# A selective-scan kernel: B products of four states at once in four row groups, and all decays in SBUF

## The chip, the cores and the metric

The kernel runs on one core of one Trainium2 chip. The metric is device time in microseconds, the median of three runs. A profiled execution is a further run with the hardware profiler on; its time and its trace are used for the parts.

## What is computed

Two layers over an image tensor of 16 x 64 x 64 x 128, in float32. Layer 0 is a two-dimensional LSTM, with a group norm ahead and a residual. Layer 1, where the change is, is a bidirectional Mamba block with the same dress. It flattens each image to 4096 tokens and runs this, once forward and once on the reversed tokens:

```python
dt, Bm, Cm = jnp.split(dbl, [DT_RANK, DT_RANK + D_STATE], axis=-1)
dt = jax.nn.softplus(dt @ dt_w.T + dt_b)
dA = jnp.exp(dt[..., None] * A)
dBx = dt[..., None] * Bm[:, :, None, :] * xc[..., None]
def step(h, inp):
    dA_t, dBx_t, C_t = inp
    h = dA_t * h + dBx_t
    return h, jnp.einsum('bds,bs->bd', h, C_t)
...
y = (ys + xc * D) * jax.nn.silu(z)
return y @ out_w.T
```

There are 256 inner channels (two halves `h` of 128 partitions) and 16 states. For each channel and state the recurrence over the tokens needs a decay `dA`, a driving term `dBx` (the "B product"), and afterwards a product with C, summed over the states.

## The kernel before

Layer 0 walks the anti-diagonals of the images. Its cell (lines 833 to 865) multiplies gates and states on VectorE, and one of these products on GpSimd (L859), with both operands in SBUF; L841, L860 and L862 are such VectorE products.

Layer 1 works in passes of T = 512 tokens: 8 chunks per direction, 16 passes per image, 256 in all. A pass holds channels in partitions and tokens in columns. ScalarE makes a decay for every state and half (`decay`, L1217: exp of dt times a per-partition scale). VectorE runs the recurrence of one state and half as one scan over 512 columns (`scan`, L1277), 32 scans per pass. A scan has two tensor operands, the decay and the driving term, and starts from `carry`, which small transfers fill (`keep`, `keep_group`).

The states are treated in two ways.

- X states (0 to 7): GpSimd multiplies dt times x (`dtx`) by rows of B spread over the partitions, for two states at a time, into an SBUF tile `group` of four states (`drive`, L1225). The decay goes to a PSUM bank `da`. The scan overwrites its part of `group`. PE turns the finished group (`turned`, L1307), ScalarE copies it out to `ht` (L1315), and PE weighs it with C (`weigh`, L1323, four column groups).
- R states (8 to 15): PE makes the driving term as a product of the turned `dtx` (`dtxt`) and a matrix `d` with rows of B on its diagonals (`drive_rows`, L1257), for two states at once, in two row groups of 64 tokens, into a PSUM tile `pair` of two banks (named `hps` in the trace). The decay goes to SBUF (`das`). The scan writes to SBUF (`hst`). GpSimd multiplies it by rows of C (`out_of`, L1300), and PE sums it (`sums`).

A pass so has 17 GpSimd products: 8 drives, 8 outs and `dtx` (`times`, L1191), each of 1024 columns.

PSUM has eight banks: four in a common store, of which at most two hold decays and two anything else (`LIMIT`), two for `pair`, which the dt projection uses as well, and two for the sum `py`. SP issues the transfers: spread rows of B and C, the matrices `d` and `k`, the scatters that fill them in DRAM, and the carries.

The order of the instructions on every engine is written out at build time. `order_of_issue` lists the operations of all passes with their dependencies and buffers, and `simulate` issues them in a model of the five queues with the durations of `COST`, the ready operation with the lowest due time (`URGENCY` plus 16 per pass) first. Scans keep the order of the string `ORDER`: a digit stands for one X state, a letter for a pair of R states. Each engine then runs its list in order; tile semaphores guard the buffers, whose numbers stand in `RINGS`.

Of the kernel before, what the change touches and what calls it, by code (L numbers as in the profile page):

```python
# [8 lines left out]
F32 = mybir.dt.float32  # L9
# [5 lines left out]
P = 128  # L15
# [21 lines left out]
GX = 4  # L37
TB = P // GX
NX = 8
NG, NR = NX // GX, (NS - NX) // 2  # L40
WD = T + P
ORDER = ("00a00b11c11d22e22f33g33h", "00a00b11c11d22e22f33g33h")


def units_of(order):

    count = {}
    for x in order:
# [3 lines left out]
        else:  # L52
# [4 lines left out]
    "bank": 4, "pair": 1, "py": 1, "das": 3, "dg": 3, "group": 3, "cd": 2, "ht": 6, "hst": 3, "hc": 4,  # L57
    "br": 3, "cr": 2, "xc": 2, "dt": 2, "dtx": 2, "dtxt": 2, "dbl": 2, "z": 1, "y": 1,
# [4 lines left out]
    "conv": 0.865, "gate": 0.87, "silu": 0.62, "softplus": 0.65, "gate_take": 0.6, "dtproj": 1.07,  # L63
    "xproj": 1.0, "xproj_take": 0.4, "times": 2.34,
    "turn": 0.47, "turn_take": 0.47, "decay": 0.62, "drive": 2.34, "drive_rows": 1.08,
    "scan": 1.18, "keep": 0.6, "keep_group": 0.6, "out": 2.34, "sums": 0.88, "skip": 0.44,
    "turned": 0.44, "turned_take": 0.47, "weigh": 1.08,
    "again": 0.88, "finish": 1.0, "finish_last": 1.2, "back": 0.47, "back_take": 0.47,
    "project": 0.95, "store_take": 0.6, "residual": 0.6, "read_load": 0.6, "read_turn": 0.47,
    "read_take": 0.5, "read_stats": 0.62, "normal": 3.0, "normalise": 0.75, "spread": 0.6, "rows": 1.2,  # L70
# [4 lines left out]
LIMIT = {"misc": 2, "bank": 2}  # L75
AHEAD = 3
ROW = 0.9
# [4 lines left out]
        {(0, 0): -5.27, (0, 1): -61.96, (0, 2): -1.51, (0, 3): -31.9, (1, 0): -36.36, (1, 1): -34.22, (1,  # L82
         2): -4.82, (1, 3): -3.48},
        {(0, 0): -13, (0, 1): -15.31, (0, 2): -17.47, (0, 3): -12.25, (1, 0): -17.78, (1, 1): -17.99, (1,
         2): -18.46, (1, 3): -13.31},
    ),
    "xproj": (
        {(): 55.58},
        {(): 50.35},
    ),  # L90
    "xproj_take": (
        {(): -34.19},
        {(): -67.81},
    ),
    "rows": (
        {(): 14.85},
        {(): 29.35},
    ),
    "dtproj": (
        {(): 21.81},  # L100
        {(): 49.19},
    ),
    "times": (
        {(): -216.85},
        {(): -50.5},
    ),
    "turn": (
        {(0,): -139.83, (1,): -112.3},
        {(0,): 38.45, (1,): 39.27},
    ),  # L110
    "turn_take": (
        {(0,): -82.61, (1,): -85.08},
        {(0,): -121.61, (1,): -124.32},
    ),
    "skip": (
        {(0,): -30.72, (1,): -29.27, (2,): -28.89, (3,): -30.37},
        {(0,): -31.71, (1,): -38.35, (2,): -27.4, (3,): -32.33},
    ),
    "spread": (
        {("b", 0): 48.76, ("d", 0): -27.02, ("c", 0): -72.82, ("b", 1): -39.91, ("k", 0): 25.29, ("d",  # L120
         1): -25.84, ("c", 1): 91.24, ("b", 2): 203.69, ("d", 2): 42.8, ("c", 2): -76.57, ("b", 3): 83.9,
         ("k", 1): -178.37, ("d", 3): 47.98, ("c", 3): -120.82},
        {("b", 0): -102.07, ("d", 0): 101.39, ("c", 0): -127.37, ("b", 1): 201.12, ("k", 0): -7.75, ("d",
         1): -16.19, ("c", 1): 237.63, ("b", 2): 27.93, ("d", 2): 187.94, ("c", 2): 178.25, ("b", 3):
         59.58, ("k", 1): 33.49, ("d", 3): -19.86, ("c", 3): 49.53},
    ),
    "drive": (
        {(0, 0): -37.87, (1, 0): -232.55, (0, 1): 70.61, (1, 1): 81.52, (2, 0): 92.85, (3, 0): -81.77,
         (2, 1): 90.65, (3, 1): -60.19},
        {(0, 0): 71.45, (1, 0): 100.65, (0, 1): 69.84, (1, 1): 238.34, (2, 0): -85.16, (3, 0): 16.29, (2,  # L130
         1): 152.24, (3, 1): 151.41},
    ),
    "decay": (
        {(0, 0): -100.09, (1, 0): -113.38, (8, 0): -17.88, (9, 0): -17.98, (2, 0): 115.94, (3, 0):
         -173.37, (8, 1): 117.83, (9, 1): 117.76, (0, 1): 117.57, (1, 1): -199.13, (10, 0): -76.99, (11,
         0): -4.35, (2, 1): -207.87, (3, 1): -174.5, (10, 1): -57.93, (11, 1): 144.9, (4, 0): -62.8, (5,
         0): 9.44, (12, 0): -249.7, (13, 0): -4.82, (6, 0): -90.12, (7, 0): -89, (12, 1): 112.66, (13,
         1): -89.33, (4, 1): -92.07, (5, 1): -92.07, (14, 0): -87.45, (15, 0): -79.99, (6, 1): -83.78,
         (7, 1): -65.02, (14, 1): -92.12, (15, 1): -92.18},
        {(0, 0): -107.74, (1, 0): 78.08, (8, 0): 64.21, (9, 0): 60.4, (2, 0): 66.94, (3, 0): -168.8, (8,  # L140
         1): -38.24, (9, 1): 83.45, (0, 1): -165.22, (1, 1): -93.49, (10, 0): -104.1, (11, 0): 17.18, (2,
         1): 7.23, (3, 1): -108.8, (10, 1): 238.21, (11, 1): -142.57, (4, 0): 16.12, (5, 0): 79.59, (12,
         0): 187.77, (13, 0): -57.05, (6, 0): 11.51, (7, 0): -45.79, (12, 1): 48.63, (13, 1): 3.55, (4,
         1): 76.92, (5, 1): 79.55, (14, 0): 84.29, (15, 0): -45.77, (6, 1): 8.28, (7, 1): 1.52, (14, 1):
         78.29, (15, 1): 80.29},
    ),
    "scan": (
        {(0, 0): -191.9, (1, 0): -180.93, (8, 0): 59.29, (9, 0): 58.95, (2, 0): 47.07, (3, 0): 1.2, (8,
         1): 43.31, (9, 1): 42.72, (0, 1): 139.84, (1, 1): 85.46, (10, 0): 88.15, (11, 0): -220.11, (2,
         1): 67.38, (3, 1): 69.08, (10, 1): 3.2, (11, 1): -48.38, (4, 0): -148.38, (5, 0): -142.6, (12,  # L150
         0): -158.76, (13, 0): -146.42, (6, 0): -147.36, (7, 0): -134.74, (12, 1): -175.53, (13, 1):
         71.17, (4, 1): 33.69, (5, 1): 137.17, (14, 0): 92.55, (15, 0): 96.04, (6, 1): 94.32, (7, 1):
         102.78, (14, 1): 86.19, (15, 1): 71.66},
        {(0, 0): -48.3, (1, 0): -50.57, (8, 0): -47.99, (9, 0): -52.26, (2, 0): -45.52, (3, 0): -48.53,
         (8, 1): -128.37, (9, 1): -157.26, (0, 1): -63.33, (1, 1): -80.02, (10, 0): -74.43, (11, 0):
         -109.52, (2, 1): -66.59, (3, 1): -80.53, (10, 1): 9.22, (11, 1): -125.5, (4, 0): -93.94, (5, 0):
         3.58, (12, 0): 2.78, (13, 0): -27.3, (6, 0): 34.58, (7, 0): 18.59, (12, 1): 6.11, (13, 1):
         12.29, (4, 1): 11.19, (5, 1): 13.36, (14, 0): 20.12, (15, 0): 47.53, (6, 1): 63.73, (7, 1):
         24.81, (14, 1): -31.39, (15, 1): -31.89},
    ),  # L160
    "scatter": (
        {("d", 0): -127.75, ("k", 0): -48.3, ("d", 1): 125.59, ("d", 2): 30.9, ("k", 1): -11.07, ("d",
         3): 59.14},
        {("d", 0): -28.6, ("k", 0): -67.41, ("d", 1): -108.16, ("d", 2): -133.73, ("k", 1): -94.37, ("d",
         3): -129.9},
    ),
    "drive_rows": (
        {(0, 0): 26.17, (0, 1): -3.25, (1, 0): -50.93, (1, 1): -31.58, (2, 0): -0.9, (2, 1): 17.32, (3,
         0): 80.19, (3, 1): -2.75},
        {(0, 0): 33.35, (0, 1): 87.4, (1, 0): -31.34, (1, 1): 14.65, (2, 0): 33.69, (2, 1): 74.37, (3,  # L170
         0): 149.93, (3, 1): -83.5},
    ),
    "keep": (
        {(0, 0): -27.42, (0, 1): -63.13, (1, 0): -50.2, (1, 1): 26.86, (2, 0): 11.68, (2, 1): 92.99, (3,
         0): -130.98, (3, 1): -233.75},
        {(0, 0): -235.44, (0, 1): 51.58, (1, 0): 122.52, (1, 1): 76.67, (2, 0): 102.66, (2, 1): -10.28,
         (3, 0): 48.92, (3, 1): -97.12},
    ),
    "out_of": (
        {(0, 0): 59.79, (0, 1): 61.42, (1, 0): -184.01, (1, 1): -237.54, (2, 0): -19.88, (2, 1): -39.04,  # L180
         (3, 0): 15.92, (3, 1): -83.32},
        {(0, 0): 46.75, (0, 1): 3.87, (1, 0): 82.21, (1, 1): 206.76, (2, 0): 148, (2, 1): -37.11, (3, 0):
         94.4, (3, 1): 76.66},
    ),
    "sums": (
        {(0, 0): 41.95, (0, 1): 68.64, (1, 0): 88.31, (1, 1): 50.57, (2, 0): 73.72, (2, 1): 76.8, (3, 0):
         -112.6, (3, 1): 161.24},
        {(0, 0): 22.75, (0, 1): 60.23, (1, 0): 33.88, (1, 1): 40.44, (2, 0): 217.19, (2, 1): 108.14, (3,
         0): 79.41, (3, 1): 83.91},
    ),  # L190
    "keep_group": (
        {(0, 0): -57.74, (0, 1): 14.03, (1, 0): 44.89, (1, 1): 61.89},
        {(0, 0): -23.9, (0, 1): -25.46, (1, 0): -99.2, (1, 1): -131.55},
    ),
    "turned": (
        {(0, 0, 0): 7.49, (0, 0, 1): -48.32, (0, 0, 2): -49.41, (0, 0, 3): 27.18, (0, 1, 0): 30.12, (0,
         1, 1): 23.21, (0, 1, 2): 38.21, (0, 1, 3): 37.84, (1, 0, 0): 60.1, (1, 0, 1): 19.71, (1, 0, 2):
         91.82, (1, 0, 3): -28.89, (1, 1, 0): 50.64, (1, 1, 1): 50.33, (1, 1, 2): 64.2, (1, 1, 3): 154.68},
# [16 lines left out]
        {(0, 0): 103.15, (0, 1): 79.93, (1, 0): 103.9, (1, 1): 79.84},  # L215
    ),
    "finish": (
        {(): -99.64},
        {(): -37.02},
    ),  # L220
    "spill": (
# [1250 lines left out]
```

## Time and profile before

| what | before |
|---|---|
| median of three runs | 14339.09 us (14334.58 to 14341.66) |
| profiled execution, its own time | 14002.73 us |
| its span | 14000.9 us |
| PE busy | 13085.1 us, 93% |
| VectorE (DVE) busy | 11100.8 us, 79% |
| ScalarE (ACT) busy | 10791.8 us, 77% |
| GpSimd (POOL) busy | 10438.0 us, 75% |
| mean granted PE clock | 0.973 |
| moved by DMA | 1936.5 MB, mean 138 GB/s |

Busy times are of one execution and overlap. Layer 0 fills roughly the first 1500 us, where GpSimd has little to do; after that the pattern of a pass repeats, and a stretch of it shows how near each engine is to the period. In a group's row stand the line, engine and operation, output and inputs with their tiles, the count, busy time and mean duration, and after the second bar the idle time of the engine just before such instructions, with what ended it. In the timeline a row has start, duration, engine, line and operation; "x2" means two merged instructions. PE's LDWEIGHTS and MATMUL are recorded separately, and a float32 product leaves two matmul records. Matmuls overlap, so the cost of one is its group's busy time by its count, not its mean duration.

### The profile page before, as it was taken

What the parts mean: (1) busy time and instruction counts of PE and PEld (TensorE: products, weight loads), DVE (VectorE), ACT (ScalarE), POOL (GpSimd) and SP (SyncE); (2) the same over time, 40 slices, a digit from 0 to 9 for tenths busy, and PEclk for the clock granted to TensorE, in tenths of its full rate; (3) what the DMA queues carried; (4) which work ended last, traced back from release to release, by engine and by line L of the source; (5) the groups of instructions that cost most, each with busy time, mean ns of one, the idle gap of its engine ahead of it and who ended that gap; (6) DMA issues with size and microseconds to landing.
All of it is one profiled execution on the core that took longest, in us unless ns stands there. A gap on an engine that the chain in (4) does not pass through costs nothing. (4 is left out here: it accounts for less than half of the span.)

```text
span 14000.9 us, 315690 instructions
## 1 busy us (share of the span) xinstructions
PE 13085.1 (93%) x124724; PEld 10060.3 (72%) x124724; DVE 11100.8 (79%) x11281; ACT 10791.8 (77%) x17599; POOL 10438.0 (75%) x4612
## 2 busy tenths in 40 slices
PE   8999899898999999998989999998989999998989
PEld 7666667676767777676767777776767677776767
DVE  6776678787887878787878888787878888787878
ACT  3444678788888878787888888788888888787877
POOL 0111488788878888887878888888878888888888
PEclk9999899999999999999999999999999999999999
DMA  4221356565555556565655555565655556565655
GB/s 144 56 57 51 84 144 156 137 152 141 152 146 147 149 144 152 137 156 141 152 142 150 149 146 147 143 158 141 151 144 153 144 149 146 143 156 142 152 141 140
DMA packets 3787992, 1936.50 MB, mean 138 GB/s; under 512 B 2938624, under 2 KB 3284240, under 8 KB 3786512
## 3 DMA queue, kind: packets, MB, share of 16 engines
q1 hardware_dynamic: 3708560, 1881.06, 53.2%
q10 hardware_dynamic: 77952, 35.24, 1.1%
q8 instruction: 986, 16.15, 0.5%
q14 instruction: 494, 4.05, 0.1%
HBM read 1754.87 MB, written 164.89 MB: 137 GB/s over the span
## 5 line engine op out<-in xcount | busy, mean ns | idle before, releaser
L1300 POOL TENSOR_TENSOR hc<-hst,cr 128x1024 f32<-128x1024 f32 x2048 | 4872.9, 2384 | 1497.8 <-DMA cr<-rows 1017.3
L1277 DVE TENSOR_TENSOR_SCAN hst<-das,carry,hps 128x512 f32<-128x512 f32 x3584 | 4376.8, 1262 | 1308.0 <-PE hps L1257 837.8
L1225 POOL TENSOR_TENSOR group<-dtx,br 128x1024 f32<-128x1024 f32 x2048 | 4898.5, 2406 | 403.3 <-DMA br<-rows 251.2
L1277 DVE TENSOR_TENSOR_SCAN group<-da,carry,group 128x512 f32<-128x512 f32 x3584 | 4393.1, 1263 | 463.9 <-ACT da L1217 324.2
L1217 ACT ACTIVATE das<-dt,A_log_sb 128x512 f32<-128x512 f32 x4096 | 2852.3, 724 | 744.5 <-DVE hst L1277 720.8
L1315 ACT COPY ht<-ptg 128x512 f32<-128x512 f32 x4096 | 2263.4, 588 | 890.9 <-PE ptg L1307 868.4
L1217 ACT ACTIVATE da<-dt,A_log_sb 128x512 f32<-128x512 f32 x4096 | 2766.5, 688 | 72.7 <-DVE group L1277 66.5
L1335 PE MATMUL py<-ident,hc 128*128 128x128 f32 x16384 | 2162.0, 281 | 495.7 <-POOL hc L1300 495.1
L1307 PE MATMUL ptg<-ident,group 128*128 128x128 f32 x16384 | 2415.1, 283 | 178.8 <-ACT ht L1315 153.6
L1257 PEld LDWEIGHTS hps<-d,dtxt 64*128 64x128 f32 x32768 | 2050.7, 192 | 636.6 <-issue 486.6
L1257 PE MATMUL hps<-d,dtxt 64*128 64x128 f32 x32768 | 2448.2, 290 | 21.8 <-ACT dt L1182 12.1
L1335 PEld LDWEIGHTS py<-ident,hc 128*128 128x128 f32 x16384 | 1869.3, 144 | 808.3 <-POOL hc L1300 532.5
L1307 PEld LDWEIGHTS ptg<-ident,group 128*128 128x128 f32 x16384 | 1820.5, 143 | 584.4 <-ACT ht L1315 252.5
L1093 PE MATMUL pp<-xT,wk 128*128 128x512 f32 x4096 | 1930.1, 609 | 0.5 <-DVE xl L880 0.5
L1093 PEld LDWEIGHTS pp<-xT,wk 128*128 128x128 f32 x4096 | 733.8, 192 | 735.1 <-issue 688.9
L859 POOL TENSOR_TENSOR a_f<-a_f,c 128x288 f32<-128x288 f32 (+40 forms) x254 | 212.7, 837 | 1331.0 <-ACT a_f L851 1265.9
L1323 PE MATMUL py<-ht,k 128*32 128x128 f32 x32768 | 1114.5, 277 | 0.3 <-ACT ht L1315 0.3
L1323 PEld LDWEIGHTS py<-ht,k 128*32 128x32 f32 x32768 | 837.4, 110 | 197.5 <-issue 177.4
L1191 POOL TENSOR_TENSOR dtx<-dt,xc 128x1024 f32<-128x1024 f32 x256 | 604.1, 2360 | 318.8 <-ACT dt L1182 291.0
L1277 DVE TENSOR_TENSOR_SCAN hst<-das,hps 128x512 f32<-128x512 f32 x512 | 595.4, 1201 | 237.0 <-PE hps L1257 201.2
L1217 ACT ACT_TABLE_LOAD x527 | 676.1, 1283 | 10.2 <-DVE hst L1277 0.4
L1277 DVE TENSOR_TENSOR_SCAN group<-da,group 128x512 f32<-128x512 f32 x512 | 596.0, 1202 | 68.9 <-ACT da L1217 63.7
(110 smaller groups left out, 11834.4 us busy)
## 6 DMA issues: line engine op xcount, KB each, us to landing
cr<-rows SPq DMA_DIRECT2D x1024, 512.0 KB
br<-rows SPq DMA_DIRECT2D x1024, 512.0 KB
d<-d SPq DMA_DIRECT2D x1024, 320.0 KB
k<-k SPq DMA_DIRECT2D x512, 256.0 KB
yf<-yo SPq DMA_DIRECT2D x128, 512.0 KB
yl<-yf SPq DMA_DIRECT2D x128, 512.0 KB
xs<-in_x_dram SPq DMA_DIRECT2D x64, 512.0 KB
d<-rows SPq DMA_DIRECT2D x2048, 2.0 KB
```

Source lines behind the costliest of these rows:

```text
L859: nc.gpsimd.tensor_mul(f0, f0, cp[:, up, :])
L1093: nc.tensor.matmul(self.ps["conv", h], lhsT=wk[:, k, h * P : (h + 1) * P], rhs=xT[self.b % 2][:, t0 : t0 + T], start=(k == 0), stop=(k == ...
L1191: nc.gpsimd.tensor_mul(self.dtx, self.dt, self.xc)
L1217: nc.scalar.activation(t, self.dt[:, h, :], AF.Exp, scale=amat[:, h, s : s + 1])
L1225: nc.gpsimd.tensor_mul(both[:, m : m + 2, :], bc(self.dtx[:, h, :], 1, 2), self.brow[q])
L1257: nc.tensor.matmul(half[:, j, :, :], lhsT=self.dtxt[rows, j, h * P : (h + 1) * P], rhs=dg[rows, j + r, :, :], start=True, stop=True, skip_ ...
L1277: nc.vector.tensor_tensor_scan(t[:, self.rev], self.da.pop((s, h))[:, self.rev], dbx[:, self.rev], 0.0 if self.first else carry[:, self.d, ...
L1300: nc.gpsimd.tensor_mul(self.hc[g, h], self.hst[g, h], self.crow[g])
L1307: nc.tensor.transpose(pt[:, k, :], self.group[g, h][:, t0 : t0 + TB, :].rearrange("p t s -> p (t s)"), ident,)
L1315: nc.scalar.copy(t, self.ps.pop(("turned", g, h, j)))
L1323: nc.tensor.matmul(self.py[q * TB : (q + 1) * TB, j // 2, c0 : c0 + P], lhsT=cd[:, GX * j + q, :], rhs=self.ht[g, h, j][:, q, :], start=False,
L1335: nc.tensor.matmul(self.py[:, j, cols], start=j not in self.banks, stop=last, skip_group_check=True, **how,)
```

## The change

The R states are taken four at a time. A product covers 32 tokens in each of four row groups and writes four states into a tile `quad` of four banks, one bank for each row group; there is one such tile. The matrices `d` have the stride of four states and are 896 columns wide, two per pass in place of four of 640. The dt projection uses two banks of `quad`.

All decays, of X states too, go to one ring of eight SBUF tiles `da`; no decay lies in PSUM. Two common banks remain. The ring `hc` has 3 tiles (4 before), `cr` 3 (2), `dg` 2 (3). The string of the order has four R states in a row between four X states (a letter now stands for one state; the drawing of four decays comes before the first). The planner's durations, the time that its model gives to transfers, and all due times are new.

```diff
-NG, NR = NX // GX, (NS - NX) // 2
-WD = T + P
-ORDER = ("00a00b11c11d22e22f33g33h", "00a00b11c11d22e22f33g33h")
+NG, NA = NX // GX, (NS - NX) // GX
+WD = T + 3 * P
+ORDER = ("00aaaa0011bbbb1122cccc2233dddd33", "00aaaa0011bbbb1122cccc2233dddd33")
...
-    "bank": 4, "pair": 1, "py": 1, "das": 3, "dg": 3, "group": 3, "cd": 2, "ht": 6, "hst": 3, "hc": 4,
-    "br": 3, "cr": 2, "xc": 2, "dt": 2, "dtx": 2, "dtxt": 2, "dbl": 2, "z": 1, "y": 1,
+    "bank": 2, "quad": 1, "py": 1, "da": 8, "dg": 2, "group": 3, "cd": 2, "ht": 6, "hst": 3, "hc": 3,
+    "br": 3, "cr": 3, "xc": 2, "dt": 2, "dtx": 2, "dtxt": 2, "dbl": 2, "z": 1, "y": 1,
...
-LIMIT = {"misc": 2, "bank": 2}
+LIMIT = {"misc": 2}
...
+                    put("drive_rows", (a, h), "PE", after=[landed, first] + turns,
+                        takes=[quad], uses=[dg, T_["dtxt"]], chain=("quad", 0))
...
+                put("scan", (s, h), "DVE", after=[get(("drive_rows", i, a, h)), get(("decay", i, s, h)), start_of(s, h)],
+                    takes=[hst] if m % 2 == 0 else [], uses=[da[s, h], quad], chain=("scan", 0))
...
-            bank = tile_of("bank")
-            da = decay(s, h, [bank], ("bank", AHEAD))
-            put("scan", (s, h), "DVE", after=[da, get(("drive", i, q, h)), start_of(s, h)],
-                uses=[bank, group], chain=("scan", 0))
+            put("scan", (s, h), "DVE", after=[decay(s, h), get(("drive", i, q, h)), start_of(s, h)],
+                uses=[da[s, h], group], chain=("scan", 0))
...
-            def decay(self, s, h, place=None):
-                if s >= NX:
-                    g, m = divmod(s - NX, 2)
-                    if m == 0:
-                        self.das[g, h] = ring(sp, "das", [P, 2, T], f"das_{self.nm}_{g}_{h}")
-                    t = self.das[g, h][:, m, :]
-                else:
-                    t = bank(place, f"da_{self.nm}_{s}_{h}")
+            def decay(self, s, h):
+                t = ring(sp, "da", [P, T], f"da_{self.nm}_{s}_{h}")
                 nc.scalar.activation(t, self.dt[:, h, :], AF.Exp, scale=amat[:, h, s : s + 1])
                 self.da[s, h] = t
...
+            def drive_rows(self, a, h):
+
+                dg = self.mat["d", a].rearrange("p (j i n) -> p j i n", n=GX, i=TB)
+                quad = psum.tile([P, GX, T], F32, name=f"hps_{self.nm}_{a}_{h}", tag="quad")
                 for j in range(NB):
-                    for r in range(NQ):
-                        rows = slice(r * step, (r + 1) * step)
-                        half = pair[:, r, :].rearrange("p (i j n) -> p j i n", j=NB, n=2)
+                    for r in range(GX):
+                        rows = slice(r * TB, (r + 1) * TB)
+                        part = quad[:, r, :].rearrange("p (i j n) -> p j i n", j=NB, n=GX)
                         nc.tensor.matmul(
-                            half[:, j, :, :],
+                            part[:, j, :, :],
                             lhsT=self.dtxt[rows, j, h * P : (h + 1) * P],
                             rhs=dg[rows, j + r, :, :],
...
-                for k in range(2):
-                    self.dbx[NX + 2 * g + k, h] = pair.rearrange("p r t -> p (r t)")[:, k::2]
+                for k in range(GX):
+                    self.dbx[NX + GX * a + k, h] = quad.rearrange("p r t -> p (r t)")[:, k::GX]
```

## The prediction

> **What bounds the kernel now.** First the busy time of one steady stretch, for the length of a pass; then its groups and waits; then the timeline of layer 0, the only place where VectorE reads two SBUF operands beside a working GpSimd.
>
> ```profile
> core 0: us, PE busy (x) PEld busy (x) DVE busy (x) ACT busy (x) POOL busy (x), PEclk, DMA share, GB/s
> 5600.00:7000.00 1400.00, 1313.39 (x13350) 1019.26 (x13347) 1137.47 (x972) 1144.13 (x1812) 1158.59 (x494) 0.98 0.58 147
> ```
>
> The stretch holds 465 decays of the X states, 16 to a pass, so 29.06 passes of 48.17 us. Per pass PE is busy 45.2 us, POOL 39.9, ACT 39.4, DVE 39.1. PE is nearest to the period; its margin is 3.0 us. The other three stand close together, so PE can give up 5 us at most before they bind.
>
> ```profile
> L1225 POOL TENSOR_TENSOR group<-dtx,br 128x1024 f32<-128x1024 f32 x233 | 557.0, 2403 | 33.4 <-DMA br<-rows 14.0 <-PE ptg L1307 8.5 <-DMA carry<-hst 5.3
> L1277 DVE TENSOR_TENSOR_SCAN group<-da,carry,group 128x512 f32<-128x512 f32 x417 | 511.2, 1263 | 54.5 <-ACT da L1217 37.0 <-POOL group L1225 9.2 <-POOL hc L1300 5.6
> L1277 DVE TENSOR_TENSOR_SCAN hst<-das,carry,hps 128x512 f32<-128x512 f32 x418 | 510.5, 1263 | 155.4 <-PE hps L1257 95.6 <-DMA carry<-hst 18.1 <-POOL group L1225 13.6
> ```
>
> Both kinds of scan take 1263 ns, and each now has one operand in PSUM: the X scan its decay `da`, the R scan its B product `hps`. While they run, GpSimd works without being slowed:
>
> ```profile
> 6011.83 2.40 POOL L1300 TENSOR_TENSOR hc<-hst,cr 128x1024 f32<-128x1024 f32 x1
> 6014.19 2.41 POOL L1225 TENSOR_TENSOR group<-dtx,br 128x1024 f32<-128x1024 f32 x1
> ...
> 6013.15 2.43 DVE L1277 TENSOR_TENSOR_SCAN hst<-das,carry,hps 128x512 f32<-128x512 f32 x2
> 6015.49 2.44 DVE L1277 TENSOR_TENSOR_SCAN group<-da,carry,group 128x512 f32<-128x512 f32 x2
> ```
>
> From start to start a scan costs 1.18 us here and a GpSimd product 2.35. In layer 0, with both operands in SBUF on both engines, it is otherwise:
>
> ```profile
> 706.44 0.87 POOL L859 TENSOR_TENSOR a_f<-a_f,c 128x312 f32<-128x312 f32 x1 [6.93 <-ACT a_f L851]
> ...
> 706.80 0.84 DVE L860 TENSOR_TENSOR a_f<-a_f,c 128x312 f32<-128x312 f32 x1 [0.20 <-ACT a_f L851]
> ...
> 708.09 0.47 DVE L862 TENSOR_TENSOR a_f<-a_f,a_f 128x312 f32<-128x312 f32 x1
> ...
> 799.28 0.54 DVE L841 TENSOR_TENSOR hs<-h 128x368 f32<-128x368 f32 x1
> ...
> 799.32 1.36 POOL L859 TENSOR_TENSOR a_f<-a_f,c 128x384 f32<-128x384 f32 x1 [5.84 <-DVE h L865]
> ```
>
> L860 needs 0.47 us alone (L862 has its shape) and takes 0.84: it ends 0.33 us after POOL, as if started 0.14 us before POOL's end. The other way round, L859 behind L841 takes 1.36 where the same shape, ahead of its neighbour at 834.15, takes 1.00: again as if started 0.14 us before the first one's end. The second waits for the whole of the first.
>
> **The change part by part**, per pass, against the profiled execution (14002.73 us, span 14000.9). Of the span, 256 x 48.17 = 12331.5 us are passes and 1669.4 layer 0 and ramps, left alone.
>
> B product. It issues 64 products before (4 pairs x 2 halves x 4 x 2) and 64 after (2 quads x 2 x 4 x 4), each 128 columns wide, so the 128 matmul records remain. A record costs 2448.2 us / 32768 = 74.7 ns in two row groups, 9.56 us per pass. Bounds: 74.7 ns (no gain) and 34.0 ns, the row of the C product, which runs in four column groups (1114.5 us / 32768). I take half of 74.7: 37.4 ns, 4.8 us saved, PE 40.4. Cover: everything below that is longer than 40.4.
>
> Decays in SBUF, ACT's side: a decay to SBUF takes 724 ns, to PSUM 688; 16 x 0.036 = 0.6 us, ACT 40.0, hidden.
>
> Decays in SBUF, VectorE's side. All 16 X scans now read two SBUF operands, `da` and `group`, beside 17 GpSimd products (8 drives, 8 outs, 1 times) that read SBUF. No scan of this kind is in the trace. One bound is no effect (the 1263 ns of both rows), the other the full blocking of layer 0; below nothing is excluded, since neither row has a cheaper scan. The Trainium skill, "SBUF — State Buffer", section "Who interferes with whom", speaks against the change: a VectorE instruction with two SBUF inputs draws the second through the interface shared with GpSimd, and the later of the two is held until the earlier is through. By the scan rows of this trace (1263 ns) the sum is below 45 us; by the rule, with layer 0's prices, it is this: a scan and a product in turn take 1.26 + 2.40 - 2 x 0.14 = 3.38 us, where the scan alone takes 1.18. A product that falls among X scans costs VectorE 2.20 us. I take the rule's side, because layer 0's delays confirm it to 0.01 us and in both orders, and the scan differs from L860 only in its operation.
>
> How many products fall there: the new order runs R and X scans in turns of four. There are 4.25 products to each such pair of turns; four R scans last 4 x 1.18 = 4.72 us and cover two products (4.70). At least 2.25 of 4.25 are left, 9 per pass. An out product needs two finished R scans, so the second out of each turn always starts as the X scans do; drives become ready after the transposes of a finished group and may slip there too. I take 10. VectorE: 32 x 1.18 + 1.15 (gate product, statistics, residual: 33.5 us in the stretch) = 38.9; plus 10 x 2.20 = 60.9 us. Ends: if nothing waits and everything alternates, products and X scans exclude each other, 39.9 + 16 x 1.18 less 9 x 0.15 = 57.4; if one more product per turn falls among X scans (3.25 x 4 = 13), 67.5. Behind a blocked X scan stand, on VectorE, the rest of its turn and the next R scans; for them wait PE's transposes, ACT's copies to `ht`, SP's carry transfers. Behind a blocked product stand the next drive and out, and so the next X scans and sums.
>
> One quad in four banks. PE can refill only when all four scans are done, and the dt projection takes the same tile. A fill costs about 16 x 2 x 37.4 ns = 1.2 us; it lies beside four X scans, 4.7 us or more. Between 0 and about 1 us per pass (the turn with the dt projection and its softplus); 0, under the blocked scans.
>
> Two banks for the rest. PE's waits on `ht` copies are 16.2 + 27.1 us in the stretch, 1.5 us per pass; between 0 and another 1.5. With PE at 40 of 61, 0.
>
> SP's queue. The d matrices become 2 x 448 KB in place of 4 x 320: 384 KB less of about 7 MB, at a DMA share of 0.58. Scatters stay at eight 2 KB transfers and carries at eight per pass. The third `cr` tile may end the wait of the out product for `cr` (111.1 us in the stretch, 3.8 per pass). If it stays, it falls where POOL has slack only if the blocking is absent; worth 0 to 3.8, taken as 0.
>
> Order of issue. It cannot shorten the blocking below 57.4. What it does to the rest lies within the 3 to 4 us that the period now stands above its longest engine.
>
> What is late next: VectorE and GpSimd, held by each other. VectorE's waits for `hps` (120.1 us, 4.1 per pass) vanish, being shorter than what replaces them.
>
> Sum: 256 x 60.9 = 15590 + 1669 = 17260 us of span. Outside the span lie 1.8 us, and the median of the runs is 336.4 above the profiled execution's own time; I carry both over: **17,600 us**. By the same steps 57.4 gives 16,700 and 67.5 gives 19,290.
>
> **The rivals.**
>
> B, not slower: the scan, at 1263 ns for 512 elements slower per element than L862 (683 ns for 504), doesn't hold what L860 and L841 hold. Place: the X scans at L1277; price 0 in place of 2.20 us. Then PE's relief counts: engines at 40.0 to 40.4 and a margin of about 4 give 44.5 us, 13,400. It decides from 48.17 - 44.5 = 3.7 us over ten meetings: below 0.37 us each the change isn't slower. For it: no row shows a scan blocked. Against it: every scan in this kernel had one PSUM operand.
>
> C: the blocking is partial, half the price, as a slow reader might leave gaps. VectorE 38.9 + 11.0, plus 3 of margin: 52.9, 15,550. Against it: layer 0 shows no halves.
>
> D: no blocking, and four row groups bring nothing (74.7 ns stays): the period stays, the single quad adds about 1 us: 14,600. For it: nothing has yet written four banks at once. Against it: two groups already halve the 147 ns of a full transpose (2415.1 us / 16384).
>
> **How the numbers follow.** The blocking (A) 0.79, B 0.11, C 0.07, D 0.03. The likeliest is 17,600, its own range 16,700 to 19,300. Of A, 0.75 lies below 19,300; with C's 0.05 above 15,000 this is 0.80: range 15,000 to 19,300. Within 0.2% is about what this kernel's measurement can't tell from no change. Faster 0.11 (B), same 0.01, slower 0.88 (A, C, most of D).
>
> **What would show it.** Right: scans `group<-da` well above 1263 ns, towards 2 us and more, while scans of `hst` stay there; GpSimd products above 2400 ns; PE busy below 75%; the B product near 37 ns a record. Wrong: `group` scans still at 1263 ns (B, or D if the records stay at 75 ns); scans near 1.8 us with no sharp steps (C). The period is wrong by size if fewer or more than ten products meet X scans, which shows as the mean of the two rows: 16 scans x excess is the price paid.

## The result, and the profile after

The changed kernel takes 17507.9 us (median of four runs, 17501.1 to 17515.1), the kernel before beside it 14340.4: a ratio of 1.220, interval [1.2177, 1.2225]. It is slower by 22%, on the side that was forecast, 0.5% below the predicted 17,600 and inside the forecast range of 15,000 to 19,300.

The groups of the page after. A row gives line, engine, operation, count, then busy time and mean duration of one, then the idle time before it with its releasers:

```profile
L1280 DVE TENSOR_TENSOR_SCAN group<-da,carry,group 128x512 f32<-128x512 f32 x3584 | 9308.9, 2650 | 31.1 <-POOL group L1228 31.1
L1228 POOL TENSOR_TENSOR group<-dtx,br 128x1024 f32<-128x1024 f32 x2048 | 6515.3, 3198 | 740.1 <-DMA br<-rows 528.1 <-PE ptg L1310 128.1 <-DVE hst L1280 31.3
L1303 POOL TENSOR_TENSOR hc<-hst,cr 128x1024 f32<-128x1024 f32 x2048 | 5787.8, 2834 | 1930.5 <-DVE hst L1280 1615.3 <-PE py L1326 95.4 <-PE ptg L1310 49.2
...
L1280 DVE TENSOR_TENSOR_SCAN hst<-da,carry,hps 128x512 f32<-128x512 f32 x3584 | 4272.7, 1249 | 8.7 <-PE hps L1260 8.5 <-issue 0.2
...
L1310 PE MATMUL ptg<-ident,group 128*128 128x128 f32 x16384 | 2744.4, 307 | 1669.6 <-DVE group L1280 1018.5 <-ACT xc L1113 508.6 <-ACT ht L1318 59.8
...
L1260 PE MATMUL hps<-d,dtxt 32*128 32x128 f32 x32768 | 1434.1, 321 | 457.5 <-DVE hst L1280 448.3 <-DMA d<-d 8.2 <-ACT dt L1191 1.0
L1280 DVE TENSOR_TENSOR_SCAN group<-da,group 128x512 f32<-128x512 f32 x512 | 1311.7, 2612 | 10.5 <-DMA k<-rows 10.5
```

One and the same scan now has two durations. Where its driving term is in PSUM (`hst`) it takes 1249 ns, as before. Where both operands are in SBUF (`group`) it takes 2650 in place of 1263. The GpSimd products have grown from 2.38 (`hc`) and 2.41 us (`group`) to 2.83 and 3.20. None of this stands in a column of waits: the blocked instruction counts as busy. VectorE sat idle for only 31.1 us before the X scans with a carry.

The busy time of a stretch after:

```profile
core 0: us, PE busy (x) PEld busy (x) DVE busy (x) ACT busy (x) POOL busy (x), PEclk, DMA share, GB/s
7000.00:8750.00 1750.00, 1296.18 (x13061) 990.22 (x13060) 1710.56 (x959) 1141.95 (x1778) 1434.99 (x480) 0.87 0.45 109
```

VectorE is busy for 98% of it, PE for 74%. A pass takes (17503.7 - 1669.4) / 256 = 61.85 us, before 48.17. The timeline shows the steps:

```profile
7999.86 4.78 DVE L1280 TENSOR_TENSOR_SCAN hst<-da,carry,hps 128x512 f32<-128x512 f32 x4
8004.55 11.02 DVE L1280 TENSOR_TENSOR_SCAN group<-da,carry,group 128x512 f32<-128x512 f32 x4
8015.49 4.76 DVE L1280 TENSOR_TENSOR_SCAN hst<-da,carry,hps 128x512 f32<-128x512 f32 x4
...
8002.38 5.60 POOL L1303 TENSOR_TENSOR hc<-hst,cr 128x1024 f32<-128x1024 f32 x2 [3.51 <-DVE hst L1280]
8007.94 6.56 POOL L1228 TENSOR_TENSOR group<-dtx,br 128x1024 f32<-128x1024 f32 x2
```

Four R scans take 4.78 us, four X scans 11.02. In those 11.02 us lie the second out product and two drives: three meetings for 6.24 us, 2.08 each. The means of the rows hide these steps: of the 4096 X scans in this trace 2885 took more than 1.6 us, 3.21 us in the mean, and the other 1211 took 1.31. That is 11.3 held scans per pass.

### The profile page after: what moved, and what is told of

The parts are those of the page before. It is cut to its first block, busy times and chain, and to the rows that moved or that the text cites. A ratio compares the mean times of both kernels' runs of the same rounds, so it can differ in the third digit from the quotient of the medians.

```text
span 17503.7 us, 315906 instructions
## 1 busy us (share of the span) xinstructions
PE 13239.0 (76%) x124724; PEld 10060.4 (57%) x124724; DVE 16646.9 (95%) x11281; ACT 10988.6 (63%) x17598; POOL 13230.1 (76%) x4612
## 5 line engine op out<-in xcount | busy, mean ns | idle before, releaser
L1280 DVE TENSOR_TENSOR_SCAN group<-da,carry,group 128x512 f32<-128x512 f32 x3584 | 9308.9, 2650 | 31.1 <-POOL group L1228 31.1
L1303 POOL TENSOR_TENSOR hc<-hst,cr 128x1024 f32<-128x1024 f32 x2048 | 5787.8, 2834 | 1930.5 <-DVE hst L1280 1615.3
L1228 POOL TENSOR_TENSOR group<-dtx,br 128x1024 f32<-128x1024 f32 x2048 | 6515.3, 3198 | 740.1 <-DMA br<-rows 528.1
L1220 ACT ACTIVATE da<-dt,A_log_sb 128x512 f32<-128x512 f32 x8192 | 5605.5, 723 | 1818.4 <-DVE group L1280 1575.6
L1280 DVE TENSOR_TENSOR_SCAN hst<-da,carry,hps 128x512 f32<-128x512 f32 x3584 | 4272.7, 1249 | 8.7 <-PE hps L1260 8.5
L1310 PE MATMUL ptg<-ident,group 128*128 128x128 f32 x16384 | 2744.4, 307 | 1669.6 <-DVE group L1280 1018.5
L1102 PE MATMUL pp<-xT,wk 128*128 128x512 f32 x4096 | 1846.8, 597 | 45.2 <-ACT ht L1318 41.6
L1260 PE MATMUL hps<-d,dtxt 32*128 32x128 f32 x32768 | 1434.1, 321 | 457.5 <-DVE hst L1280 448.3
L1260 PEld LDWEIGHTS hps<-d,dtxt 32*128 32x128 f32 x32768 | 1214.2, 220 | 873.4 <-DVE hst L1280 552.4
L1280 DVE TENSOR_TENSOR_SCAN group<-da,group 128x512 f32<-128x512 f32 x512 | 1311.7, 2612 | 10.5 <-DMA k<-rows 10.5
L1338 PE MATMUL py<-ddiag,xc 128*128 128x128 f32 x4096 | 678.6, 325 | 139.5 <-DVE y L1393 134.7
L1338 PEld LDWEIGHTS py<-ddiag,xc 128*128 128x128 f32 x4096 | 627.0, 236 | 167.4 <-DVE y L1393 144.1
```

The costliest lines, as they stand in the source:

```text
L1102: nc.tensor.matmul(self.ps["conv", h], lhsT=wk[:, k, h * P : (h + 1) * P], rhs=xT[self.b % 2][:, t0 : t0 + T], start=(k == 0), stop=(k == ...
L1220: nc.scalar.activation(t, self.dt[:, h, :], AF.Exp, scale=amat[:, h, s : s + 1])
L1228: nc.gpsimd.tensor_mul(both[:, m : m + 2, :], bc(self.dtx[:, h, :], 1, 2), self.brow[q])
L1260: nc.tensor.matmul(part[:, j, :, :], lhsT=self.dtxt[rows, j, h * P : (h + 1) * P], rhs=dg[rows, j + r, :, :], start=True, stop=True, skip_ ...
L1280: nc.vector.tensor_tensor_scan(t[:, self.rev], self.da.pop((s, h))[:, self.rev], dbx[:, self.rev], 0.0 if self.first else carry[:, self.d, ...
L1303: nc.gpsimd.tensor_mul(self.hc[g, h], self.hst[g, h], self.crow[g])
```

## The experiments

The theory is that an X scan whose two operands both lie in SBUF and a GpSimd product that reads SBUF exclude each other. The rivals are that the scan is slower by itself with two SBUF operands, that both engines only share bandwidth, and that the loss comes from the rest of the change: the single quad, two common banks, the order. Unless said otherwise a ratio is to the kernel before, run beside it.

**One part of the change alone.** The kernel before, with the X decays in SBUF (two tiles):

```diff
-                    t = bank(place, f"da_{self.nm}_{s}_{h}")
+                    t = sp.tile([P, T], F32, name=f"da_{self.nm}_{s}_{h}", tag="dax", bufs=2)
```

> The kernel before with one thing of the change alone: the decays of the X states go to SBUF (two tiles) in place of the common PSUM banks; pairs, order and everything else stay. Theory (X scans with two SBUF operands and GpSimd products exclude each other, 2.20 us per product that falls among X scans): turns of two R scans cover about one product, so again some 9 to 11 products per pass meet X scans; X scans at 2.4 to 2.7 us in the mean, R scans still near 1.25, time 16,900 to 18,000 us. Rival (the loss comes from the single quad, the two common banks or the new order): 14,200 to 14,600 us, X scans at 1.26.

Measured 17156.9 us, ratio 1.226 [1.2228, 1.2285]. Its groups:

```profile
L1277 DVE TENSOR_TENSOR_SCAN group<-da,carry,group 128x512 f32<-128x512 f32 x3584 | 8685.3, 2461 | 40.3 <-ACT da L1217 39.4
...
L1277 DVE TENSOR_TENSOR_SCAN hst<-das,carry,hps 128x512 f32<-128x512 f32 x3584 | 4348.7, 1252 | 469.1 <-PE hps L1257 414.1 <-POOL dtx L1191 39.0 <-issue 16.0
...
L1277 DVE TENSOR_TENSOR_SCAN group<-da,group 128x512 f32<-128x512 f32 x512 | 1183.8, 2350 | 4.3 <-ACT da L1217 3.5
```

This one line brings the whole loss, with pairs, four banks and the old order in place. The rival that laid it to the rest of the change falls.

**The change without this part.** In the changed kernel an X scan reads one operand from a PSUM bank of constants. The bank is won by laying the two banks of `py` over each other. Leaving the decay out of the scan also removes the scan's wait for it.

```diff
+        xk = psum.tile([P, T], F32, name="xk", tag="xk")
+        nc.vector.memset(xk, 0.5)
...
-                    self.py = psum.tile([P, NB // 2, 2 * DI], F32, name=f"py_{self.nm}", tag="py")
+                    self.py = psum.tile([P, 1, 2 * DI], F32, name=f"py_{self.nm}", tag="py")
...
-                    self.da.pop((s, h))[:, self.rev],
+                    (xk if s < NX else self.da[s, h])[:, self.rev],
```

> The changed kernel with one operand of every X scan back in PSUM: it reads a constant bank in place of its decay (the decays are still made in SBUF; the bank comes from the sum py, whose two banks are laid over each other, with the same work), so its output isn't the reference's. Quad, order, two common banks stay. Theory: X scans back at 1.25 us, the period is set by four engines near 40 us each plus 3 to 6 us, 43.5 to 46.5 us per pass, 12,900 to 13,900 us; PE's relief then shows. Rival (quad, banks, order cost the time): above 16,500 us. Second rival (no port, but PE not relieved by four row groups): 14,200 to 14,700.

Measured 13792.9 us, ratio 0.985 [0.9833, 0.9868].

```profile
L1282 DVE TENSOR_TENSOR_SCAN group<-xk,carry,group 128x512 f32<-128x512 f32 x3584 | 4328.6, 1262 | 49.5 <-POOL group L1230 49.5
...
L1282 DVE TENSOR_TENSOR_SCAN hst<-da,carry,hps 128x512 f32<-128x512 f32 x3584 | 4310.7, 1259 | 1548.9 <-DMA carry<-hst 572.6 <-PE hps L1262 335.5 <-DMA carry<-group 156.1
```

The busy time of a stretch of this run:

```profile
core 0: us, PE busy (x) PEld busy (x) DVE busy (x) ACT busy (x) POOL busy (x), PEclk, DMA share, GB/s
6000.00:8000.00 2000.00, 1742.27 (x19271) 1331.82 (x19268) 1624.71 (x1412) 1657.08 (x2623) 1665.45 (x709) 0.95 0.57 140
```

The X scan is back at 1262 ns and the loss is gone, in the upper part of the expected range. PE's relief shows as busy time (87% of the stretch), but hardly as time.

**GpSimd that doesn't read.** Both operands of the X scan stay in SBUF; each drive and each out multiplies 16 of 1024 columns and fills the rest.

```diff
+CUT = 8
...
+        def part(o, x, y):
+            nc.gpsimd.tensor_mul(o[:, :, :CUT], x[:, :, :CUT], y[:, :, :CUT])
+            nc.gpsimd.memset(o[:, :, CUT:], 0.01)
...
-                nc.gpsimd.tensor_mul(self.hc[g, h], self.hst[g, h], self.crow[g])
+                part(self.hc[g, h], self.hst[g, h], self.crow[g])
```

> The changed kernel with decays and order as they are, but each GpSimd product of the drives and outs multiplies 16 of its 1024 columns only and fills the rest with a constant, which reads nothing; the output isn't the reference's. Theory: a fill reads no SBUF and holds nothing, so X scans fall to 1.25 to 1.35 us though both their operands stay in SBUF; 12,300 to 13,900 us. Rival (a scan with two SBUF operands is slower by itself, GpSimd or not): X scans stay at 2.6 us, 17,000 us or more. Second rival (any GpSimd work beside it slows the scan, writes too): between, in proportion to the length of the fills.

Measured 13246.5 us, ratio 0.946 [0.9435, 0.9491].

```profile
L1286 DVE TENSOR_TENSOR_SCAN group<-da,carry,group 128x512 f32<-128x512 f32 x3584 | 4349.8, 1271 | 28.1 <-POOL group L1081 27.3 <-ACT da L1226 0.7
```

1271 ns with two SBUF operands: the scan isn't slower by itself. GpSimd was busy filling beside it, so neither its presence nor its writes are the cause. The time lies inside the expected range, and 546 us below the run with the constant operand: the fills also leave GpSimd with less work (busy for 8034.0 us in place of 10437.4).

**The dose.** The same with `CUT = 256`, half of each product:

> The changed kernel with 512 of the 1024 columns of each drive and out multiplied and the other half filled with a constant (the output isn't the reference's). Dose: if a product holds what a scan needs for as long as it reads, a meeting costs half, some 1.0 to 1.1 us; ten of them put VectorE at 38.9 + 10.5 = 49 to 50 us per pass, which is above everything else: 14,200 to 15,000 us, X scans at 1.7 to 1.95 us. If the price were a fixed one per meeting, whatever the length of the product, X scans stay near 2.6 us and 17,000 us.

Measured 14769.2 us, ratio 1.056 [1.0534, 1.0577]; and these rows for the X scans, with and without a carry:

```profile
L1286 DVE TENSOR_TENSOR_SCAN group<-da,carry,group 128x512 f32<-128x512 f32 x3584 | 6783.7, 1946 | 29.3 <-POOL group L1081 29.3
...
L1286 DVE TENSOR_TENSOR_SCAN group<-da,group 128x512 f32<-128x512 f32 x512 | 878.5, 1767 | 9.0 <-POOL group L1081 9.0
```

Half the reading costs about half: (14763.4 - 1669.4) / 256 = 51.1 us per pass, within the expected time and 1 us above the expected 49 to 50. A fixed price per meeting falls. Nor did the number of meetings change much: 10.8 X scans per pass took more than 1.6 us (11.3 in the changed kernel), now 2.25 us in the mean.

**The cost by itself.** A kernel of nothing but 16 scans, 16 GpSimd instructions or both per stage, executed once:

```diff
+nc.vector.tensor_tensor_scan(t, das, t, 0.0, ALU.mult, ALU.add)   # L43, L50, L62, L68, L76
+nc.vector.tensor_tensor_scan(t, dap, t, 0.0, ALU.mult, ALU.add)   # L56, dap in PSUM
+nc.gpsimd.tensor_mul(hc[i % 2], a, b)                             # L46 alone, L52, L58; L73 half
+nc.gpsimd.memset(hc[i % 2], 0.25)                                 # L64
+nc.gpsimd.tensor_scalar_mul(hc[i % 2], a, 0.5)                    # L70
```

> The disputed cost by itself; nothing of the reference is computed. Stages of 16 scans and 16 GpSimd instructions, parted by small exchanges: scans with both operands in SBUF alone; GpSimd products of 1024 columns alone; both together; the scan's decay in PSUM beside products; both in SBUF beside fills; beside one-operand multiplications; beside products of 512 columns. Theory: alone 1.20 us a scan; beside products of 1024 columns they take turns, 3.3 to 3.4 us from scan to scan, products also 3.3 to 3.4; with the decay in PSUM 1.20 and 2.40; beside fills 1.20; beside one-operand multiplications they take turns too; beside products of 512 columns about 2.2. Rival (bandwidth is shared in parts): beside products both engines slow by less than the sum, 1.7 to 2.6 us from scan to scan with no steps.

```profile
L52 POOL TENSOR_TENSOR hc<-a,b 128x1024 f32<-128x1024 f32 x16 | 50.6, 3200 | 0.0
L50 DVE TENSOR_TENSOR_SCAN g<-das,g 128x512 f32<-128x512 f32 x16 | 47.4, 3035 | 0.0
...
L58 POOL TENSOR_TENSOR hc<-a,b 128x1024 f32<-128x1024 f32 x16 | 37.1, 2350 | 0.0
L46 POOL TENSOR_TENSOR hc<-a,b 128x1024 f32<-128x1024 f32 x16 | 36.8, 2341 | 0.0
...
L76 DVE TENSOR_TENSOR_SCAN g<-das,g 128x512 f32<-128x512 f32 x16 | 32.3, 2092 | 0.0
L68 DVE TENSOR_TENSOR_SCAN g<-das,g 128x512 f32<-128x512 f32 x16 | 23.5, 1546 | 0.0
L62 DVE TENSOR_TENSOR_SCAN g<-das,g 128x512 f32<-128x512 f32 x16 | 18.0, 1204 | 0.0
L43 DVE TENSOR_TENSOR_SCAN g<-das,g 128x512 f32<-128x512 f32 x16 | 18.0, 1200 | 0.0
L56 DVE TENSOR_TENSOR_SCAN g<-dap,g 128x512 f32<-128x512 f32 x16 | 17.9, 1201 | 0.0
```

Alone a scan takes 1200 ns (L43), with its decay in PSUM beside the products 1201 (L56), beside fills 1204 (L62). Beside products with both operands in SBUF the mean is 3035 (L50), but it holds two kinds of scan: the first two began before the first product did and took 1.2 us; from then on every scan is held. Two rows with the shortest, the median and the longest scan in ns, then, from the timeline, the end of that stage and two pieces of the stage with one-operand multiplications:

```profile
L50 DVE TENSOR_TENSOR_SCAN g<-das,g x16: 1201/3295/3302, 69.0 to 113.0; 128x512 f32<-128x512 f32 x16
...
L76 DVE TENSOR_TENSOR_SCAN g<-das,g x16: 1202/2217/2225, 225.3 to 255.4; 128x512 f32<-128x512 f32 x16
...
74.44 41.89 DVE L50 TENSOR_TENSOR_SCAN g<-das,g 128x512 f32<-128x512 f32 x13
...
181.97 3.06 POOL L70 TENSOR_SCALAR hc<-a 128x1024 f32<-128x1024 f32 x1
182.38 2.00 DVE L68 TENSOR_TENSOR_SCAN g<-das,g 128x512 f32<-128x512 f32 x1
...
184.30 1.20 DVE L68 TENSOR_TENSOR_SCAN g<-das,g 128x512 f32<-128x512 f32 x1
```

A held scan takes 3.30 us, so from scan to scan it is (41.89 - 3.30) / 12 = 3.22, against 17.96 / 16 = 1.12 alone and 36.8 / 16 = 2.30 for a product. They take turns: the cycle is the sum of both less 0.20 us, a little below the expected 3.3 to 3.4 and well above the 1.7 to 2.6 of shared bandwidth. A meeting costs 3.22 - 1.12 = 2.10 us; with products of half the length (L76) a held scan takes 2.22 us, 1.02 more than alone in place of 2.10. One part of the theory missed: a multiplication with one SBUF operand (L70) held only every second scan, which took 2.00 us; the scan between took 1.20, beside the same kind of instruction. The mean of 1546 ns is of these two.

**The rings alone.** The kernel before with two ring sizes of the change, `cr` 3 and `hc` 3:

```diff
-    "bank": 4, "pair": 1, "py": 1, "das": 3, "dg": 3, "group": 3, "cd": 2, "ht": 6, "hst": 3, "hc": 4,
-    "br": 3, "cr": 2, "xc": 2, "dt": 2, "dtx": 2, "dtxt": 2, "dbl": 2, "z": 1, "y": 1,
+    "bank": 4, "pair": 1, "py": 1, "das": 3, "dg": 3, "group": 3, "cd": 2, "ht": 6, "hst": 3, "hc": 3,
+    "br": 3, "cr": 3, "xc": 2, "dt": 2, "dtx": 2, "dtxt": 2, "dbl": 2, "z": 1, "y": 1,
```

> The kernel before with the changed kernel's two rings alone: cr 3 tiles (2), hc 3 (4); the order follows from the same due times. It asks what the prediction put at 0 to 3.8 us per pass, the wait of the out product for cr. If the wait sets part of the period, 13,400 to 14,200 us; if PE at 45.2 of 48.2 us sets it, or the fourth hc tile is worth as much, 14,200 to 14,600.

Measured 13820.7 us, ratio 0.987 [0.9855, 0.9889]. That is nearly as much as the changed kernel gained without its X decays (0.985), whose `cr` and `hc` are the same. It fits that its other parts come to little together; each by itself wasn't tried. Among the longest waits of this run, in a stretch of 2000 us, is this (total, times, longest in us):

```profile
POOL group L1225 <- DMA br<-rows: 103.3, 19, 8.6
```

With `cr` there in time GpSimd next waits for the rows of B. So these got a fourth tile (`"br": 4`):

> The kernel before with the two rings of the change (cr 3, hc 3) and a fourth tile for the spread rows of B, on which the drives wait in the run with the two rings alone (103 us in 2000). If GpSimd's waits for rows set the period, a further 100 to 300 us below that run, 13,500 to 13,750; if the wait only moves on to another place, within 50 us of it.

Measured 13678.2 us, ratio 0.977 [0.9757, 0.9789]: faster than both kernels, with the X decays where they were.

**Two attempts that brought nothing.** First, the fourth `br` tile in the changed kernel with the constant PSUM operand (`"br": 4`, `"da": 6`):

> The run with the X scans' operand in a constant PSUM bank again (output not the reference's), with a fourth tile for the rows of B and six tiles da in place of eight. It asks why PE's relief brought so little there. If the rows of B were late, 13,300 to 13,600 us; if carries, refills of the single quad and the planned order hold the period, within 60 us of 13,793.

Measured 13962.3 us, ratio 0.998 [0.9969, 0.9988], worse than without (13792.9) and outside both expectations. The rows of B are off the list of its longest waits, and decays, softplus and `pz` stand there instead; which of the two ring sizes did it isn't settled, and so this run doesn't say why PE's relief brought so little. Then the changed kernel's planned durations (`COST`) in the kernel with the three rings:

> As the kernel before with cr 3, hc 3, br 4, and the changed kernel's planned durations, which lie nearer to the measured rows (scan 1.22, drive 2.40, turned copy 0.555). The due times are those of before. Better durations give an order that fits: up to 150 us less than without; but due times found for other durations may lose as much: 13,500 to 14,000 us.

Measured 14237.7 us, ratio 1.018 [1.016, 1.0191], 4% slower than with the old durations and outside the range. Here due times that were found for one set of durations didn't carry over to another, though it lay nearer to the measured rows.

**The two blocked kernels side by side.** The changed kernel once more, and with it the kernel before with the X decays in SBUF:

> The changed kernel as it is, beside the kernel before on one chip together with the next run. The kernel before took 14,340 us beside the changed one and 14,000 us in the later calls, so the 336 us that the prediction carried over are the chip's. If they go with the chip whatever the kernel, the changed kernel takes 17,070 to 17,250 us where before takes 14,000; if they go with PE (which is no bound after the change), 17,450 to 17,550.

> The kernel before with the X decays in SBUF alone, again, on the same chip as the changed kernel. If the rest of the change (quad, rings, banks, order) is worth nothing while the blocking sets the period, the two lie within 150 us of each other; if PE's relief still counts, the changed kernel is faster by more; if the turns of four cost meetings, slower by more.

Measured 17482.4 and 17135.3 us, with the kernel before at 13999.2 (ratios 1.248 [1.2448, 1.2521] and 1.224 [1.2201, 1.2272]). With the kernel before at 14,000 the changed one stays near its first 17,508: the second of the two cases expected of it. It is 347 us slower than the one edit alone. Its X scans are longer: per pass, 16 x (10620.6 - 9869.1) / 4096 = 2.9 us, from the busy times of the two `group` rows of the first profiled execution of each (with and without carry). Part comes back elsewhere: R scans wait 8.7 us for `hps` and the like before them, with the one edit alone 469.1 (rows above). More X scans are held: 11.3 per pass took more than 1.6 us, against 9.9 with the one edit alone, both at 3.2 us in the mean. That turns of four meet more products than turns of two fits this, but the order wasn't tried by itself.

## Why the prediction was right

**The blocking.** The step that decided was to take the rule's side and layer 0's delays for an operation that the trace of before showed only with an operand in PSUM. The runs bear it out from five sides: the edit alone, the operand back in PSUM, products that don't read, half the dose, and the bare measurement.

**Price and number.** The prediction had ten meetings of 2.20 us, 22.0 us per pass. The X scans' busy time is (9308.9 + 1311.7) / 4096 = 2.593 us each; above 1.18 that makes 16 x 1.41 = 22.6. Of its two factors the price was a little too dear (2.10 measured by itself, 2.08 in the timeline) and the count a little low (11.3 held scans per pass), and these two errors nearly cancel. Layer 0's overlap of 0.14 us nearly holds for the scan too: a scan's record alone and a product's, 1.20 + 2.34, exceed the cycle of 3.22 by twice 0.16. VectorE was busy for 1710.56 / 28.25 = 60.55 us per pass (the stretch has 904 decays, 32 to a pass), against the predicted 60.9. Its idle time, (1750 - 1710.56) / 28.25 = 1.4, was not in the sum; with it the pass comes to 61.95 us in this stretch and to 61.85 over all.

**What was carried over.** Here two errors cancel, and that is luck: either alone would have put the number 1.4 to 1.9% off. The span came to 17503.7 us where the sum said 17,260, 244 too low; and the 336 us between the profile and the runs of before, which I added, aren't there after the change (17505.5 of its own time, median 17507.9). The kernel before took 14,340 us beside the changed one and 13,990 to 14,000 on three later occasions, while the changed kernel took 17,508 and 17,482. So the 336 us belonged to the occasion, and of these two only the kernel before, in which PE is busy for 93%, felt it. Nor is it a matter of the chip: a single execution of the kernel before took 14,428 us on the chip on which it took 13,999 soon after. Why isn't shown.

**The B product.** Predicted 37.4 ns a record, measured 1434.1 / 32768 = 43.8 at a clock of 0.869, and 38.0 (1244.9 us) in the run with the constant operand at 0.958. The halving came as taken only in the second. And PE's whole busy time per pass, put at 40.4 us, was 1296.18 / 28.25 = 45.9 in the changed kernel, no less than the 45.2 before: its other products took longer too (a record of the group's transposes 2744.4 us / 16384 = 168 ns in place of 147, at the lower clock). Under a VectorE of 60.55 us this cost nothing.

**The rivals.** B's mechanism is refuted, and its price was wrong too: without any blocking the change gives 13,793 us where before takes 14,001, while the same steps say 13,061 with the 338 us left out. Failed is the step that read PE, busiest at 45.2 of 48.2 us, as what the period would follow. With the constant operand (42.2 passes of (13789.8 - 1669.4) / 256 = 47.35 us in the stretch) PE's busy time fell to 1742.27 / 42.2 = 41.2 us per pass, and the period only to those 47.35; the rings alone give 47.49. What took PE's place isn't settled. The R scans there wait longest for carries (572.6 us), then for refills of `hps` (335.5); with less work on GpSimd, in the run with fills, the period is (13222.7 - 1669.4) / 256 = 45.1. C's half price is not found: held scans take the full 3.2 us. Nor is D's unchanged record.

**The wait for `cr`,** taken as 0 under the blocking and 0 to 3.8 us without it, is worth (14001 - 13821) / 256 = 0.7 us per pass in the kernel before, where nothing blocks; this takes in the loss of one `hc` tile. Under the blocking it wasn't tried by itself.

## What to carry to other kernels

Before moving an operand, ask from which memory each operand of the instruction then comes and who works beside it: a scan that GpSimd didn't hold with one operand in PSUM made the whole kernel 22 to 25% slower with both in SBUF. The profile doesn't show such blocking as a wait, so look for one instruction with two durations and for busy shares that rise without more work. And the busiest engine isn't yet the bound: here 4 us less of PE, together with a third tile for rows that arrive late, moved the period by less than 1 us, and that tile (with one `hc` tile fewer) moved it nearly as much without PE's relief.

## What the runs showed that was not expected

Not every GpSimd read blocks alike: multiplications with two SBUF operands, 2.34 us long alone, made every scan 2.10 us later; those with one, 2.76 us long after the scans had ended, held every second scan for 0.8 us and let the other pass. A GpSimd fill of 1008 columns took 943 ns into `hc` and 2006 into `group`, whose columns have a stride of four (the stride wasn't tried by itself); the products of both cost the same (2389 and 2406 ns in the run with the constant operand). PE's mean granted clock was lower in the runs in which PE was busy for less of the span: 0.973 at 93% before, 0.958 at 88% with the constant operand, 0.923 at 82% with the one edit, 0.869 at 76% after. Why isn't shown here.
